# The last layer of a four-layer graph network: neighbours summed first, the first group's four parts in turn, output by node residue

## Chip, cores, metric

One core of a Trainium2 chip. In the views PE is TensorE's matmuls, PEld its weight loads, DVE VectorE, ACT ScalarE and POOL GpSimd.

## The reference

Four graph layers run over x of 128 graphs x 64 nodes x 256 features, each as layernorm(x + layer(x)). The change touches only the fourth:

```python
h = relu(einsum('ts,bsh->bth', adj, x @ Wg0 + bg0))
h = relu(einsum('ts,bsh->bth', adj, h @ Wg1 + bg1))
for p in range(1, 5):               # an LSTM over windows of p nodes
    nw   = 64 // p
    last = lstm_last(Wih[p-1], Whh[p-1], ..., h[:, :nw*p].reshape(-1, p, 256))
    h    = h.at[:, arange(nw)*p + p-1].set(last)
x = layernorm(x + h)
```

The sum over neighbours (`adj`) and the product with `Wg0` are linear, so adj (x Wg0 + bg0) = (adj x) Wg0 + rowsum(adj) bg0. The neighbours may be summed first.

After p = 3, nodes 0, 1 and 2 of every four are final. Only node 3 of every four is still written, by p = 4.

## The kernel before

Layer 3 (the fourth) runs in eight groups of 16 graphs. A group's graph convolution is a generator `gcn(g, a)` with four parts, a = 0 to 3, of 256 rows (4 graphs) each. Its steps are handed out one by one beside the LSTM of the group before. `bdT` is the adjacency, transposed, twice on a diagonal. x3, the layernorm's result, lies in a buffer that the views call A. Cuts are marked `# ...`.

```python
def gcn(g, a):
    # ... load x2r; z = A * sc2 + sh2 (ScalarE)
    # transpose z (L753), x2r += z (L754), layernorm on GpSimd -> x3 (L96), x3 to DRAM
    yield
    p_ = gbank([KD, 2, P])
    for k in range(KD):
        for c in range(2):
            nc.tensor.transpose(p_[:, k, c, :], x3[:, c, k*P:(k+1)*P], ident)      # L764
    hT = work.tile([P, KD, HT], F32, name="hT")
    nc.vector.tensor_copy(hT, p_.rearrange("p k c t -> p k (c t)"))
    yield
    for n in range(2):
        # hT x wg[n], 128x256 (L772); + bg[n] -> y (VectorE)
        yield
        # y x bdT, 128x128 (L780); relu -> hT (n = 0) or H (n = 1, L789)
        yield
GCN_STEPS = 6

def final(g):                                # four output tiles, by time
    # ... for a in range(4): load x3r, transpose H (L859), add, layernorm, store
    yield

for _ in steps_of(0):                        # first group: parts (0,1), then (2,3)
    pass
for g in range(NG):
    ending = final(g - 1) if g else iter(())
    side = steps_of(g + 1) if g + 1 < NG else iter(())
    n_side, done = halves * GCN_STEPS, 0     # 24
    for u, _ in enumerate(lstm(g)):          # 22 units: p = 1: 4, p = 2: 4, p = 3: 6, p = 4: 8
        next(ending, None)
        while done < min(n_side, (u + 1) * n_side / (n_units - 2)):
            next(side, None); done += 1
for _ in final(NG - 1):
    pass
```

## Time and profile before

| | before |
|---|---|
| time, median of 3 runs | 2362.1 us (2361.1 to 2364.0) |
| span of the profiled run | 2361.3 us |
| TensorE busy | 95% |
| end of layer 2 | 896.3 us |
| start: from there to the first LSTM matmul | 51.8 us |
| groups 0 to 6, start to start | 171.6, 178.1, 176.4, 178.1, 176.4, 178.1, 178.1 us |
| last group, to its last hidden state | 152.1 us |
| tail: from there to the end | 24.1 us |

The group starts are where the first 512-column LSTM matmul begins in the trace of TensorE.

### The profile page before, as it was taken

How to read it: one execution, taken by the hardware profiler on the slowest of the kernel's cores; microseconds unless marked ns; L12 is line 12 of the kernel's file. 1: busy time of each engine (PE TensorE's matmuls, PEld its weight loads, DVE VectorE, ACT ScalarE, POOL GpSimd, SP SyncE). 2: the span in 40 equal slices, each digit the busy share in tenths (PEclk: the TensorE clock that was granted, in tenths of full speed). 3: DMA queues.
4: the chain of work that ended last, by engine and by line, in shares of the span. 5: the costliest groups of instructions: out<-in, count | busy, mean ns of one | idle time of the engine just before them, and what ended most of it. 6: DMA issues, size and time to landing. Idle time of an engine off the chain costs nothing.

```text
span 2361.3 us, 25955 instructions
## 1 busy us (share of the span) xinstructions
PE 2239.4 (95%) x9673; PEld 1541.9 (65%) x9673; DVE 1019.8 (43%) x2320; ACT 910.8 (39%) x1885; POOL 408.1 (17%) x531
## 2 busy tenths in 40 slices
PE   5999999999899996999999999999999999999996
PEld 3767787778654444568568568568568568568475
DVE  5676766776744434322422422422422422422322
ACT  2565665566433801333333333333333333323331
POOL 1013333223320001010210210210210210210101
PEclk8899999999999997999999999999999999999998
DMA  3020222122223003000100100100100100100100
GB/s 119 10 38 29 46 57 39 38 46 39 30 47 90 0 0 116 18 18 1 54 18 1 54 18 1 54 19 1 54 18 1 54 18 1 45 10 1 36 1 27
DMA packets 126797, 74.75 MB, mean 32 GB/s; under 512 B 81872, under 2 KB 117328, under 8 KB 126416
## 3 DMA queue, kind: packets, MB, share of 16 engines
q1 hardware_dynamic: 124032, 70.22, 12.1%
q10 hardware_dynamic: 1616, 1.84, 0.2%
q8 instruction: 76, 1.25, 0.2%
q0 software_dynamic: 1024, 1.05, 0.2%
q14 instruction: 49, 0.40, 0.1%
HBM read 44.51 MB, written 28.57 MB: 31 GB/s over the span
## 4 chain that ended last, share of the span: by engine, by line
PE 87%; DVE 6%; ACT 3%; DMA 2%; POOL 2%; issue 1%; SPq 0%; POOLq 0%; ACTq 0%; DVEq 0%
PE l L818 32%; PE l L824 18%; PE g L772 5%; PE pz L680 5%; PE pz L616 5%; PE e L277 3%; PE g L780 2%; PE m L252 2%; PE m L365 2%; PE m L187 2%; PE z L286 2%; PE m L255 2%; PE m L377 1%; PE m L166 1%; DVE lo L290 1%
## 5 line engine op out<-in xcount | busy, mean ns | idle before, releaser
L818 PE MATMUL l<-H,wih 128*128 128x256 f32 (+2 forms) x2496 | 801.1, 472 | 0.3 <-DVE H L789 0.2
L818 PEld LDWEIGHTS l<-H,wih 128*128 128x128 f32 x2496 | 467.3, 191 | 246.2 <-issue 158.8
L824 PE MATMUL l<-hid,whh 128*128 128x256 f32 (+2 forms) x1536 | 435.9, 437 | 0.0
L824 PEld LDWEIGHTS l<-hid,whh 128*128 128x128 f32 x1536 | 291.8, 190 | 128.4 <-issue 61.2
L830 ACT ACTIVATE gate_i<-l,bias 128x256 f32<-128x256 f32 (+2 forms) x176 | 100.3, 570 | 646.2 <-PE l L824 514.9
L833 DVE TENSOR_TENSOR gate_i<-gate_i,gate_g 128x256 f32<-128x256 f32 (+2 forms) x96 | 47.8, 498 | 571.1 <-ACT gate_g L830 571.1
L834 POOL TENSOR_TENSOR cell<-gate_f,cell 128x256 f32<-128x256 f32 (+2 forms) x96 | 83.7, 872 | 1018.2 <-ACT gate_f L830 1018.2
L290 DVE SCALAR_TENSOR_TENSOR lo<-z,hi 128x512 fp32r<-128x512 f32 x256 | 167.4, 679 | 63.2 <-ACT hi L289 62.2
L289 ACT ACTIVATE hi<-z 128x512 fp32r<-128x512 f32 x256 | 143.7, 598 | 102.6 <-PE z L286 98.6
L82 POOL TENSOR_TENSOR ln_rs<-ln_rs,mhalf 128x2 f32<-128x2 f32 (+1 forms) x96 | 86.8, 904 | 520.3 <-DVE ln_ng L94 520.2
L830 ACT ACTIVATE gate_g<-l,bias 128x256 f32<-128x256 f32 (+2 forms) x176 | 100.2, 570 | 108.1 <-PE l L818 59.0
L830 ACT ACTIVATE gate_o<-l,bias 128x256 f32<-128x256 f32 (+2 forms) x176 | 99.5, 565 | 71.4 <-PE l L824 54.0
L277 PE MATMUL e<-lo,apad 128*128 128x512 f32 x256 | 110.7, 432 | 14.0 <-DVE lo L290 14.0
L772 PE MATMUL g<-wg,hT 128*128 128x256 f32 x512 | 122.6, 384 | 0.0
L286 PE MATMUL z<-gath_r,qs 128*128 128x512 f32 x256 | 109.9, 481 | 8.1 <-DVE lo L290 8.0
L837 DVE TENSOR_TENSOR cell<-gate_i,gate_g 128x512 f32<-128x512 f32 (+2 forms) x80 | 48.4, 604 | 154.6 <-ACT gate_g L830 154.5
L772 PEld LDWEIGHTS g<-wg,hT 128*128 128x128 f32 x512 | 98.3, 194 | 23.7 <-issue 10.5
L616 PE MATMUL pz<-A,w 128*128 128x512 f32 x256 | 112.7, 596 | 0.0
L277 PE MATMUL e<-hi,apad 128*128 128x512 f32 x256 | 108.3, 423 | 2.4 <-ACT hi L289 2.3
L838 ACT ACTIVATE gate_g<-cell 128x256 f32<-128x256 f32 (+2 forms) x176 | 89.9, 511 | 51.3 <-DVE cell L837 36.8
L843 DVE TENSOR_TENSOR H<-gate_o,gate_g 128x512 f32<-128x512 f32 (+2 forms) x80 | 47.6, 595 | 106.1 <-PE l L818 90.1
L616 PEld LDWEIGHTS pz<-A,w 128*128 128x128 f32 x256 | 48.2, 191 | 56.2 <-issue 55.0
(197 smaller groups left out, 2798.5 us busy)
## 6 DMA issues: line engine op xcount, KB each, us to landing
xin<-in_x SPq DMA_DIRECT2D x16, 512.0 KB
ld<-table SPq DMA_DIRECT2D x16, 512.0 KB
x_dram<-x SPq DMA_DIRECT2D x16, 512.0 KB
x2r<-x_dram SPq DMA_DIRECT2D x32, 256.0 KB
x_dram<-A SPq DMA_DIRECT2D x64, 128.0 KB
x3r<-x_dram SPq DMA_DIRECT2D x64, 128.0 KB
out<-st SPq DMA_DIRECT2D x64, 128.0 KB
wih<-in_WihT SPq DMA_DIRECT2D x3, 1024.0 KB
```

Source lines behind the costliest of these rows:

```text
L82: nc.gpsimd.tensor_tensor(dst, dst, mhalf[:, :n], OP.pow)
L277: nc.tensor.matmul(pes[S], apad[:, k, P - HEADS - r0:2 * P - HEADS - r0], t, start=first and n == 0, stop=False)
L286: nc.tensor.matmul(z, L1[q]["qs"][c][:, s, k * P:(k + 1) * P], gath_r, start=True, stop=True)
L289: nc.scalar.activation(hi, z, AF.Relu)
L290: nc.vector.scalar_tensor_tensor(lo, z, 0.0, hi.bitcast(F32), op0=OP.max, op1=OP.subtract)
L616: nc.tensor.matmul(p_, w1[:, k, m * P:(m + 1) * P], A[:, q, k * QT:(k + 1) * QT], start=k == 0, stop=k == KD - 1)
L680: nc.tensor.matmul(p_, w2[:, k, m * P:(m + 1) * P], hidden(q, k), start=k == 0, stop=k == M1 - 1)
L772: nc.tensor.matmul(p_[:, c, :], hT[:, k, c * P:(c + 1) * P], wg[n][:, k, :], start=k == 0, stop=k == KD - 1)
L818: nc.tensor.matmul(gates[n], wih[p][:, k, mw * P:(mw + 1) * P], Hw[:, k, :, s, :], start=k == 0, stop=not s and k == KD - 1)
L824: nc.tensor.matmul(gates[n], whh[p][:, k, m * P:(m + 1) * P], hid[:, k], start=False, stop=k == KD - 1)
L830: nc.scalar.activation(act[n], gates[n], AF.Tanh if n == "g" else AF.Sigmoid, bias=bias[:, p - 1, m:m + 1])
L838: nc.scalar.activation(act["g"], cell[:, j], AF.Tanh)
```

## The change

The intent has three parts. Drop the four transposes of x3 by multiplying with `bdT` first: a matmul with x3 as the stationary operand both sums neighbours and transposes (a part's eight records take 0.89 us within the groups). Run the first group's four parts in turn, where TensorE would otherwise wait for each pair. Put out three quarters of each group during its own p = 4 stage, so that one tile is left at the end. Cut to its core:

```diff
+    rb = we.tile([P, KD, 2, P], F32, name="rb")          # rowsum(adj) * bg0
+    ones = we.tile([P, P], F32, name="ones")
+    nc.vector.memset(ones, 1.0)
+    pr = gbank([P])
+    nc.tensor.matmul(pr, ones, bdT, start=True, stop=True)
...
-                nc.tensor.transpose(p_[:, k, c, :], x3[:, c, k * P:(k + 1) * P], ident)
+                nc.tensor.matmul(p_[:, k, c, :], x3[:, c, k * P:(k + 1) * P], bdT, start=True, stop=True)
+        hT = work.tile([P, KD, HT], F32, name="hT", bufs=3)
...
+                nc.tensor.matmul(p_[:, m, :], wg[0][:, k, m * P:(m + 1) * P], hT[:, k, :], ...)
+        nc.vector.tensor_add(hT, p_, rb.rearrange("p k c t -> p k (c t)"))
+        nc.scalar.activation(hT, hT, AF.Relu)
...                                     # then wg[1] and bdT as before
-    GCN_STEPS = 6
+    GCN_STEPS = 5
...
-    def final(g):
+    def final(g, s, pieces=1):          # the nodes s of every four
+        # s = 3: h is the last LSTM's own output; else GpSimd copies it out of H
...
-            parts = [gcn(g, a), gcn(g, a + 1)]
+        n = 2 if g else halves
+            parts = [gcn(g, a + m, gbank if g or m % 2 else lbank) for m in range(n)]
...
+            if u == 0 and g:
+                final(g - 1, SKIP - 1)
+            s, odd = divmod(u - first4, 2)          # u = 14, 16, 18
+            if not odd and 0 <= s < SKIP - 1:
+                final(g, s)
...
-    for _ in final(NG - 1):
-        pass
+    final(NG - 1, SKIP - 1, pieces=2)
```

`gbank` hands out the PSUM banks of the convolution, `lbank` those of the LSTM, which are free before the first group.

More of the change, by code (lines that the diff above doesn't have):

```diff
@@ L84, in layernorm @@
     def layernorm(dst, src, n, engine):
-        st = small.tile([P, n, 6], F32, name=f"ln_st{n}")
-        mv = small.tile([P, n, 2], F32, name=f"ln_mv{n}")
-        ng = small.tile([P, n], F32, name=f"ln_ng{n}")
-        rs = small.tile([P, n], F32, name=f"ln_rs{n}")
+        st = small.tile([P, n, 6], F32, name="ln_st", bufs=6)
+        mv = small.tile([P, n, 2], F32, name="ln_mv", bufs=6)
+        ng = small.tile([P, n], F32, name="ln_ng", bufs=6)
+        rs = small.tile([P, n], F32, name="ln_rs", bufs=6)
         for r in range(n):
@@ L644 @@
         wg = [weights(wd, f"wg{n}", i[f"L3_gnn_Wg{n}"]) for n in range(2)]
-        bg = [bcast(wd, f"bg{n}", i[f"L3_gnn_bg{n}"]) for n in range(2)]
+        bg0 = vec("bg0", i["L3_gnn_bg0"], KD)
+        bg1 = bcast(wd, "bg1", i["L3_gnn_bg1"])
         wih, whh = {}, {}
@@ L736, in gbank, with lbank, gcn @@
         return ps.tile([P] + shape, F32, name="g", bufs=3)
-    Hs = {}
-    def gcn(g, a):
+    def lbank(shape):
+        return ps.tile([P] + shape, F32, name="l", bufs=5)
+    rb = we.tile([P, KD, 2, P], F32, name="rb")
[3 more added lines that the diff above has]
+    nc.tensor.matmul(pr, ones, bdT, start=True, stop=True)
+    for k in range(KD):
+        for c in range(2):
+            nc.vector.tensor_scalar_mul(rb[:, k, c, :], pr, bg0[:, k:k + 1])
+    Hs, lasts = {}, {}
+    def gcn(g, a, bank):
         q, hf = divmod(g * halves + a, 2)
@@ L749, in gcn @@
                                  bias=sh2[:, m:m + 1], scale=sc2[:, m:m + 1])
-        p_ = gbank([2, D])
-        for c in range(2):
-            for m in range(KD):
+        p_ = bank([2, D])
+        for m in range(KD):
+            for c in range(2):
                 nc.tensor.transpose(p_[:, c, m * P:(m + 1) * P], z[:, m, c * P:(c + 1) * P], ident)
@@ L760, in gcn @@
         yield
-        p_ = gbank([KD, 2, P])
+        p_ = bank([KD, 2, P])
+        for c in range(2):
+            for k in range(KD):
+                nc.tensor.matmul(p_[:, k, c, :], x3[:, c, k * P:(k + 1) * P], bdT, start=True, stop=True)
+        hT = work.tile([P, KD, HT], F32, name="hT", bufs=3)
+        nc.vector.tensor_copy(hT, p_.rearrange("p k c t -> p k (c t)"))
+        yield
+        p_ = bank([KD, HT])
+        for m in range(KD):
+            for k in range(KD):
+                nc.tensor.matmul(p_[:, m, :], wg[0][:, k, m * P:(m + 1) * P], hT[:, k, :],
+                                 start=k == 0, stop=k == KD - 1)
@@ new lines, in gcn @@
+        hT = work.tile([P, KD, HT], F32, name="hT", bufs=3)
+        nc.vector.tensor_add(hT, p_, rb.rearrange("p k c t -> p k (c t)"))
+        nc.scalar.activation(hT, hT, AF.Relu)
+        yield
+        p_ = bank([2, D])
+        for c in range(2):
+            for k in range(KD):
+                nc.tensor.matmul(p_[:, c, :], hT[:, k, c * P:(c + 1) * P], wg[1][:, k, :],
+                                 start=k == 0, stop=k == KD - 1)
+        y = work.tile([P, 2, D], F32, name="st", bufs=5)
@@ L762, in gcn @@
+        nc.vector.tensor_add(y, p_, bg1[:, None, :].to_broadcast([P, 2, D]))
+        yield
+        p_ = bank([KD, 2, P])
         for k in range(KD):
             for c in range(2):
-                nc.tensor.transpose(p_[:, k, c, :], x3[:, c, k * P:(k + 1) * P], ident)
-        hT = work.tile([P, KD, HT], F32, name="hT")
-        nc.vector.tensor_copy(hT, p_.rearrange("p k c t -> p k (c t)"))
-        yield
-        for n in range(2):
-            p_ = gbank([2, D])
-            for c in range(2):
-                for k in range(KD):
-                    nc.tensor.matmul(p_[:, c, :], hT[:, k, c * P:(c + 1) * P], wg[n][:, k, :],
-                                     start=k == 0, stop=k == KD - 1)
-            y = work.tile([P, 2, D], F32, name="st", bufs=5)
-            nc.vector.tensor_add(y, p_, bg[n][:, None, :].to_broadcast([P, 2, D]))
-            yield
-            p_ = gbank([KD, 2, P])
-            for k in range(KD):
-                for c in range(2):
-                    nc.tensor.matmul(p_[:, k, c, :], y[:, c, k * P:(k + 1) * P], bdT, start=True, stop=True)
-            if n == 0:
-                hT = work.tile([P, KD, HT], F32, name="hT")
-                nc.vector.tensor_scalar_max(hT, p_.rearrange("p k c t -> p k (c t)"), 0.0)
-            else:
-                if g not in Hs:
-                    Hs[g] = work.tile([P, KD, N, GB], F32, name="H")
-                dst = Hs[g].rearrange("p k t b -> p k b t")[:, :, a * 4:(a + 1) * 4, :]
-                nc.vector.tensor_scalar_max(dst, p_.rearrange("p k c (s t) -> p k (c s) t", s=2), 0.0)
-            yield
@@ L792 @@
-    GCN_STEPS = 6
+                nc.tensor.matmul(p_[:, k, c, :], y[:, c, k * P:(k + 1) * P], bdT, start=True, stop=True)
+        if g not in Hs:
+            Hs[g] = work.tile([P, KD, N, GB], F32, name="H")
+        dst = Hs[g].rearrange("p k t b -> p k b t")[:, :, a * 4:(a + 1) * 4, :]
+        nc.vector.tensor_scalar_max(dst, p_.rearrange("p k c (s t) -> p k (c s) t", s=2), 0.0)
+        yield
+    GCN_STEPS = 5
     def lstm(g):
@@ L806, in lstm @@
                     last = s == p - 1
-                    new = None if last else work.tile([P, KD, nww, GB], F32, name="hid")
+                    over = last and p < SKIP
+                    if over:
+                        new = None
+                    elif last:
+                        new = work.tile([P, KD, nww, GB], F32, name="hd", bufs=3)
+                    else:
+                        new = work.tile([P, KD, nww, GB], F32, name="hid")
                     ends = []
@@ L842, in lstm @@
                             for jj, o, t in ends:
-                                nc.vector.tensor_mul(Hw[:, jj, :, s, :] if last else new[:, jj], o, t)
+                                nc.vector.tensor_mul(Hw[:, jj, :, s, :] if over else new[:, jj], o, t)
                         yield
                     hid = new
-    def final(g):
-        H = Hs.pop(g).rearrange("p k t b -> p k (t b)")
-        rows = [v[g * GB:(g + 1) * GB].rearrange("b (c t) d -> c t b d", t=TC) for v in (x3_dram, out_view)]
-        for a in range(halves):
-            xr = work.tile([P, 2, D], F32, name="x3r")
-            for c in range(2):
-                nc.sync.dma_start(xr[:, c, :], rows[0][2 * a + c])
+        lasts[g] = hid
@@ new lines, in final @@
+    def final(g, s, pieces=1):
+        if s == SKIP - 1:
+            h = lasts.pop(g)
+        else:
+            h = work.tile([P, KD, N // SKIP, GB], F32, name="hd", bufs=3)
+            nc.gpsimd.tensor_copy(h, Hs[g].rearrange("p k (w s) b -> p k w s b", s=SKIP)[:, :, :, s, :])
+        h = h.rearrange("p k w b -> p k (w b)")
+        rows = [v[g * GB:(g + 1) * GB].rearrange("b (c w s) d -> s c w b d", c=2, s=SKIP)[s]
+                for v in (x3_dram, out_view)]
+        xr = work.tile([P, 2, D], F32, name="x3r")
+        for c in range(2):
+            nc.sync.dma_start(xr[:, c, :], rows[0][c])
+        o = work.tile([P, 2, D], F32, name="st", bufs=5)
+        for cs in ([(0, 1)] if pieces == 1 else [(0,), (1,)]):
@@ L855, in final @@
             p_ = gbank([2, D])
-            for c in range(2):
-                t0 = (2 * a + c) * P
+            for c in cs:
                 for k in range(KD):
-                    nc.tensor.transpose(p_[:, c, k * P:(k + 1) * P], H[:, k, t0:t0 + P], ident)
-            nc.vector.tensor_add(xr, p_, xr)
-            o = work.tile([P, 2, D], F32, name="st", bufs=5)
-            layernorm(o, xr, 2, nc.gpsimd)
-            for c in range(2):
-                nc.sync.dma_start(rows[1][2 * a + c], o[:, c, :])
@@ L865, in final @@
-            yield
+                    nc.tensor.transpose(p_[:, c, k * P:(k + 1) * P], h[:, k, c * P:(c + 1) * P], ident)
+            r = slice(cs[0], cs[-1] + 1)
+            nc.vector.tensor_add(xr[:, r], p_[:, r], xr[:, r])
+            layernorm(o[:, r], xr[:, r], len(cs), nc.gpsimd)
+            for c in cs:
+                nc.sync.dma_start(rows[1][c], o[:, c, :])
     def steps_of(g):
-        for a in range(0, halves, 2):
-            parts = [gcn(g, a), gcn(g, a + 1)]
+        n = 2 if g else halves
@@ L871, in steps_of @@
+        for a in range(0, halves, n):
+            parts = [gcn(g, a + m, gbank if g or m % 2 else lbank) for m in range(n)]
             for _ in range(GCN_STEPS):
@@ L878 @@
     n_units = sum(-(-(N // p) // (QT // GB)) * p * KD for p in range(1, SKIP + 1))
+    first4 = n_units - SKIP * KD
     for g in range(NG):
-        ending = final(g - 1) if g else iter(())
         side = steps_of(g + 1) if g + 1 < NG else iter(())
@@ L884 @@
         for u, _ in enumerate(lstm(g)):
-            next(ending, None)
+            if u == 0 and g:
[3 more added lines that the diff above has]
+                final(g, s)
             while done < min(n_side, (u + 1) * n_side / (n_units - 2)):
```

## The prediction

> **What bounds the kernel now.** I read the page first, then the chain of work that ended last in order of time, then TensorE's waits, then the table by stretch. Shares say TensorE:
>
> ```profile
> PE 2239.4 (95%) x9673; PEld 1541.9 (65%) x9673; DVE 1019.8 (43%) x2320; ACT 910.8 (39%) x1885; POOL 408.1 (17%) x531
> PE 87%; DVE 6%; ACT 3%; DMA 2%; POOL 2%; issue 1%; SPq 0%; POOLq 0%; ACTq 0%; DVEq 0%
> ```
>
> An average does not say what the change is worth, since it touches only layer 3, which starts where layer 2's last matmul (L680) ends, at 896.3 us. In order of time, layer 3 has three parts. A *start* from 896.3 to 948.1, with no LSTM yet: four parts of the first group go through the graph convolution in two pairs. Then eight *groups* of LSTM, whose first matmuls begin at 948.1, 1119.9, 1298.0, 1474.5, 1652.6, 1829.0, 2007.2 and 2185.3. Last a *tail*, from the last hidden state at 2337.2 to 2361.3. The start, from the chain:
>
> ```profile
> 897.91 9.11 DMA x2r<-x_dram
> ...
> 914.59 4.52 PE g L772 x16
> 919.11 1.94 PE g L780 x16
> 921.05 3.46 PE g L772 x16
> 924.51 2.01 PE g L780 x16
> ...
> 932.96 1.11 POOL A L96 x2
> ...
> 947.01 1.04 DVE H L789
> ```
>
> The reader is to see that the second pair (from about 926) runs the whole chain again, with its own wait for GpSimd's normalisation, and that the same 16 records cost 4.52 us after a pause and 3.46 later. Within a group TensorE is nearly full, so what matters there is matmul time and holes. The chain gives the unit costs (two records per f32 matmul, one per transpose), and the waits give the one hole:
>
> ```profile
> 1202.11 0.89 PE g L780 x8
> ...
> 1221.96 0.44 PE g L764 x4
> ...
> 1240.92 1.73 PE g L772 x8
> ```
>
> ```profile
> PE g L764 <- POOL A L96: 9.6, 5, 1.9
> ```
>
> That is the wait table from 1145 on; a sixth such wait of 1.9 us falls at 1133. Each sits near a group's start, where the scheduler put the transposes of x3 (L764) only about 2.5 us behind those of z (L753), while the residual add, the statistics and GpSimd's normalisation take 5.5 us. The hole costs more than itself. In the table by stretch around four of the six holes:
>
> ```profile
> 1134.00:1145.00 11.00, 10.14 (x29) 5.30 (x30) 6.39 (x20) 3.27 (x5) 5.84 (x9) 0.84 0.44 131
> 1311.00:1322.00 11.00, 9.09 (x31) 4.70 (x31) 7.45 (x24) 3.40 (x6) 7.23 (x11) 1.00 0.49 142
> 1489.00:1500.00 11.00, 10.57 (x30) 5.51 (x31) 6.09 (x20) 3.27 (x5) 5.30 (x10) 0.84 0.46 143
> 1665.00:1676.00 11.00, 9.09 (x31) 4.51 (x30) 8.01 (x28) 3.96 (x7) 7.14 (x10) 1.00 0.47 141
> ```
>
> After the window come its length, then PE busy; the clock is the third number from the end. Where it is 0.84, the same work takes more PE time. The groups agree: from start to start they last 178.1, 176.4, 178.1, 176.4, 178.1 and 178.1 us, the long ones being those with a lowered clock (0.84 twice above; the other two show 0.84 and 0.86). So the drop costs 1.7 us, in four of six.
>
> [...]
>
> **The change, part by part.** The order of instructions up to layer 2's end is the same in both kernels but for one tiny load, so 896.3 stays.
>
> *Neighbours first.* Per part (256 rows) the old path has 4 transposes of z, 4 of x3, 8 wide matmuls and 8 matmuls with bdT. The new one multiplies x3 by bdT directly, which sums and transposes at once: 4 transposes, 8 wide, 8 with bdT. Exactly the 4 transposes of L764 go: 0.44 us. VectorE loses one 128x512 pass (0.69 us) and ScalarE gains a Relu, both beside TensorE. Seven groups of parts (those for groups 1 to 7) lie on TensorE's path: 7 x 4 x 0.44 = 12.4 us.
>
> *The holes.* In the new order the z transposes of a first part are followed by 2 LSTM matmuls, the second part's transposes and 6 more (1.72 + 0.44 + 5.15 = 7.3 us) before x3 is used, against the 5.5 us needed; only one output tile is at work then, not four. I expect the holes and drops to go: 6 x 1.9 + 4 x 1.7 = 18.2 us.
>
> *Four parts in turn.* TensorE reaches x3 of the first part at 911.3 as now. GpSimd's normalisations come every 1.86 us (0.70 + 1.10 and gaps), so the fourth is done near 917.4, its bdT matmuls at 918.0. Then 4 x 1.73 (wg0) + 4 x 1.73 (wg1) + 4 x 0.89 (bdT) = 17.4, plus some 1.2 for the cold clock (4.52 against 3.46), ends at 936.6; VectorE's four writes of H at 1.04 to 1.07 us, begun at 934.2, end at 938.4. The LSTM starts there, not at 948.1: 9.7 us. Buffers: three hT make a copy wait for the first wg0 product, which TensorE's 1.73 us per part covers.
>
> *Output by residue.* Three of a group's four output tiles move into its own p = 4 stage. The count is the same, but three of group 0 now lie within the counted groups: 3 x 0.44 = 1.3 us lost. The larger effect is the tail. Before:
>
> ```profile
> 2337.26 0.56 PE g L859 x3
> ...
> 2346.04 4.03 DMA x3r<-x_dram
> ...
> 2356.16 0.54 POOL st L96
> ```
>
> Four tiles, the later two waiting for x3r, because two buffers are reloaded only after the first outputs: 24.0 us from the hidden state to the end. After: one tile in two halves, its x3r loaded long before. Transposes and add 0.9, statistics and the two small operations 0.85, power and normalisation 1.25 give 3.0 for the first half, 4.3 for the second (one more GpSimd power and normalisation), then 4.6 from the last normalisation to the end as now (2356.7 to 2361.3): 8.9 us. Gain 15.1.
>
> *Sum:* 12.4 + 18.2 + 9.7 - 1.3 + 15.1 = 54.1; 2362.1 - 54.1 = 2308.0 us.
>
> **Rivals.** *Holes move.* In the new order the filler between the last p = 3 product and the first p = 4 product is 0.89 us of bdT work instead of 1.73, and a residue copy on GpSimd must end before the transposes behind the first p = 4 unit. For it: a hole of 1 us in seven groups with a clock drop in four costs about 14 us, giving 2322. Against: in the last group, which has no filler at all there, 2288.5 to 2297.45 holds 8.64 us of matmuls, a stall of 0.3 us; and the permuting copy of 128x1024 took 2.03 us, so 128x512 is estimated at 1.0 us, with 3.5 us from the p = 3 end to its use. ScalarE's Relu could also wait for VectorE and hold back gates, but ScalarE is 33% busy in these groups.
>
> *Only matmul time goes.* If the holes persist in another place and the start is bound by the GpSimd chain with a cold clock throughout (gain 6), it is 12.4 - 1.3 + 6 + 15 = 32, or 2330: within 2%. For it: holes depend on a scheduler's order, which I judge by arithmetic. Against: the 2 us of margin.
>
> *The start is limited by the loads.* x2r lands at 907 because weights go ahead of it on the same queue; it still does, and parts 3 and 4 might come later than I think. The DMA rate falls off after 908, so all four loads should be there by 910, and this is hidden behind GpSimd's rate.
>
> **Range and chances.** 2% faster is 2314.9, so I have 7 us in hand. The tail (15) and the transposes (12) are almost certain, the start sure to 3 us; the 18 us of holes carry the doubt. Half of them surviving gives 2317. Better than 2300 needs slack that I do not see: the records of a full group alone (LSTM 147.9: 136 records of 512 columns at 0.429, 152 of 336 at 0.283, 216 of 256 at 0.216; convolution 4 x 5.68; output 1.7) come to 172.3 us, against 176.4 - 1.9 - 1.8 = 172.7 in my sum. Range 2300 to 2320; faster 0.8, same 0.19, slower 0.01.
>
> **What would show it.** Group length 172 to 173 us, all alike, with no TensorE wait on A at group starts and the clock at 1.00 there; first LSTM matmul near 938; no L764-like transposes; tail near 9 us with no DMA wait in it. Groups of 174 or more, or waits on hd or H at the p = 4 start, would show the first rival. A start above 942 would break the part-in-turn step.

## More of the kernel before

The metric is device microseconds of one execution.

The prediction shows the lines for the start, the waits and the tail, so here is only one hole in detail. The view is TensorE's timeline in the kernel before; columns are start, length, engine, line and operation. The profile models where a matmul ends, and lengths run into the next start (1308.32 plus 0.60 is past 1308.76), so differences of starts say more.

```profile
1306.88 0.75 PE L753 MATMUL g<-ident,st 128*128 128x128 f32 x4
1307.46 1.02 PE L818 MATMUL l<-H,wih 128*128 128x512 f32 x2
1308.32 0.60 PE L753 MATMUL g<-ident,st 128*128 128x128 f32 x4
1308.76 1.02 PE L818 MATMUL l<-H,wih 128*128 128x512 f32 x2
1309.62 0.60 PE L859 MATMUL g<-ident,H 128*128 128x128 f32 x4
1310.06 1.02 PE L818 MATMUL l<-H,wih 128*128 128x512 f32 x2
1312.99 0.33 PE L764 MATMUL g<-ident,A 128*128 128x128 f32 x1 [1.91 <-POOL A L96]
```

The z transposes of the first part are issued by 1307.46. The x3 transposes, which need VectorE's add and statistics and GpSimd's normalisation first, start at 1312.99, 5.53 us later. Only 3.62 us of TensorE work stand between, so TensorE idles 1.91.

## The result

2309.8 us median (2308.6 to 2310.3, 4 runs) against 2362.0 on the same chip. The ratio is 0.9777, 95% interval 0.976 to 0.9794: faster, by 2.2%. Ratios are the mean of one kernel's runs over the mean of the other's in the same rounds, so not quite the ratio of the medians. The predicted time was 2308.0.

From the page of the changed kernel, busy times and the chain's shares:

```profile
PE 2217.8 (96%) x9547; PEld 1526.4 (66%) x9547; DVE 1000.6 (43%) x2296; ACT 928.2 (40%) x1917; POOL 417.9 (18%) x556
PE 89%; DVE 5%; ACT 3%; DMA 1%; POOL 1%; issue 1%; SPq 0%; POOLq 0%; ACTq 0%; DVEq 0%
```

TensorE still sets the time, with 21.6 us less of busy time. The start, from the chain of work:

```profile
911.29 0.57 POOL A L96
...
911.90 2.08 PE l L779 x8
913.98 1.86 PE g L779 x8
915.84 1.77 PE l L779 x8
917.61 1.13 PE g L779 x8
918.74 1.73 PE l L786 x8
...
933.49 3.72 DVE H L808 x4
...
937.25 7.99 PE l L844 x18
```

There is one run through the convolution where the kernel before had two. The four bdT products start 1.86 us apart, as GpSimd's normalisations do, and from 918.74 TensorE runs without a gap. TensorE's waits from 940 to the end (waited for, total, times, longest):

```profile
PE g L893 <- DVE hd L869: 1.4, 1, 1.4
PE l L844 <- ACT gate_g L864: 0.5, 1, 0.5
```

The six waits for A are gone. The first of these two lies in the tail and the second at 2168.7, in the last group. One of the stretches where z and x3 stand now, in the table by stretch (PE busy comes after the length, the clock is the third number from the end):

```profile
1118.00:1129.00 11.00, 11.00 (x39) 5.86 (x38) 6.74 (x19) 5.90 (x11) 4.80 (x8) 1.00 0.44 131
```

TensorE is busy for all 11 us, at full clock. The tail, from the chain:

```profile
2299.10 0.44 DVE hd L869
...
2302.37 0.56 POOL st L96
2302.92 0.52 POOL ln_rs L82
```

No read of x3r is left in it. By part, from the two profiled runs:

| part | predicted gain | before | after | measured gain |
|---|---|---|---|---|
| end of layer 2 | 0 | 896.3 | 896.7 | -0.4 |
| start | 9.7 | 51.8 | 40.6 | 11.2 |
| group 0 (4 x 0.44, less 1.3) | 0.5 | 171.6 | 171.7 | -0.1 |
| groups 1 to 6 (transposes 10.6, holes and clock 18.2) | 28.8 | 1065.4 | 1038.0 | 27.4 |
| last group | 0 | 152.1 | 152.5 | -0.4 |
| tail | 15.1 | 24.1 | 8.3 | 15.8 |
| sum | 54.1 | 2361.3 | 2307.9 | 53.4 |

The parts are rounded one by one.

### The profile page after: what moved, and what is told of

The parts are those of the page before. It is cut to its first block, busy times and chain, and to the rows that moved or that the text cites.

```text
span 2307.9 us, 25661 instructions
## 1 busy us (share of the span) xinstructions
PE 2217.8 (96%) x9547; PEld 1526.4 (66%) x9547; DVE 1000.6 (43%) x2296; ACT 928.2 (40%) x1917; POOL 417.9 (18%) x556
## 4 chain that ended last, share of the span: by engine, by line
PE 89%; DVE 5%; ACT 3%; DMA 1%; POOL 1%; issue 1%; SPq 0%; POOLq 0%; ACTq 0%; DVEq 0%
PE l L844 33%; PE l L850 18%; PE pz L681 5%; PE pz L616 5%; PE e L277 3%; PE m L252 2%; PE m L187 2%; PE m L365 2%; PE g L786 2%; PE g L795 2%; PE z L286 2%; PE m L255 2%; PE m L377 1%; PE g L779 1%; PE m L166 1%; PE g L803 1%
## 5 line engine op out<-in xcount | busy, mean ns | idle before, releaser
L82 POOL TENSOR_TENSOR ln_rs<-ln_rs,mhalf 128x2 f32<-128x2 f32 (+2 forms) x97 | 84.5, 871 | 544.1 <-DVE ln_ng L94 543.4
L869 DVE TENSOR_TENSOR H<-gate_o,gate_g 128x512 f32<-128x512 f32 (+1 forms) x64 | 40.9, 639 | 87.7 <-PE l L844 70.1
L856 ACT ACTIVATE gate_f<-l,bias 128x256 f32<-128x256 f32 (+2 forms) x96 | 51.1, 532 | 60.2 <-PE l L850 60.2
L263 DVE TENSOR_TENSOR qs<-m,qs 64x256 fp32r<-64x256 f32 x128 | 53.9, 422 | 48.2 <-ACT qs L262 46.2
```

What stands on the lines that cost most here:

```text
L82: nc.gpsimd.tensor_tensor(dst, dst, mhalf[:, :n], OP.pow)
L856: nc.scalar.activation(act[n], gates[n], AF.Tanh if n == "g" else AF.Sigmoid, bias=bias[:, p - 1, m:m + 1])
```

## The experiments

Theory: the gain is a sum of four causes that can be undone one by one. These are the x3 transposes, the start in one run, the tail with one tile, and holes closed by wider spacing of the side steps. The main rival concerns the holes: they went because the output tiles went away, or because of the convolution's new form. The runs were made on several chips: beside them the kernel before took 2360.9 us (first four runs below), 2361.7 (next four) and 2358.3 (last two), so differences of a few us between chips are read from the parts of the profiles and not from the times.

### The old kernel with another spacing

```diff
-            while done < min(n_side, (u + 1) * n_side / (n_units - 2)):
+            while done + 1 <= min(n_side, (u + 1) * n_side / (n_units - 2)):
```

> The kernel before with one thing changed: the side steps of the next group's convolution are handed out with the count rounded down (one step beside the first LSTM unit, not two), so x3 of the first part is used some 8 us of TensorE work after its z transposes, not 2.5. Theory (the holes at group starts are a matter of spacing, and each drop of the clock follows from a hole): the six holes of 1.9 us and the four clock drops of 1.7 us go, groups last 174.5 us all alike, time 2362 - 18 = 2344 us. Rival (the holes come from four output tiles crowding VectorE and GpSimd there): holes of at least 1 us remain, time 2352 or more.

Measured: 2346.0 us, ratio 0.9931 (0.9914 to 0.9947). Groups 1 to 6 last 174.6 or 174.7 us each, 17.5 us less in sum than before, and between the groups' first and last starts TensorE waits for nothing but 0.2 us at the first LSTM matmul. The steps keep their rate, and each comes later by up to one unit. TensorE's timeline:

```profile
1131.35 1.88 PE L818 MATMUL l<-H,wih 128*128 128x512 f32 x4
...
1139.53 0.60 PE L764 MATMUL g<-ident,A 128*128 128x128 f32 x4
```

x3 is used 8.2 us after the z transposes, and nothing waits, with all four output tiles in place. One line of the old kernel thus gives what I had booked under the change. The profiled run is 15.8 us shorter than that of the kernel before, not 17.5, because it left layer 2 at 897.4, took 52.2 us for its start and 0.6 more for group 0, and 0.4 less for its tail; the medians differ by 14.9.

### Neighbours first alone, at two spacings

Both are the kernel before with the new convolution in it, the first group in pairs and the old output. The second also keeps the old rate:

```diff
-            while done < min(n_side, (u + 1) * n_side / (n_units - 2)):
+            while done < min(n_side, (u + 1) * 24 / (n_units - 2)):
```

> The kernel before with only the neighbours-first convolution (five steps per part, so also one side step per LSTM unit), first group in pairs and output as before. Theory: 28 parts x 0.44 = 12.4 us of transposes go from the groups, some 2 us from the start's two pairs, and the holes and clock drops (18 us) go because five steps are spaced wider: 2362 - 32 = 2330 us, groups 172.7 us. Rival (the holes need the output moved away): holes stay, 2348 us.

> As e2, but the side steps at the old rate of 1.2 per LSTM unit. Theory (spacing): x3 of the first part is used some 3.5 us after its z transposes again, the holes of about 2 us come back with some clock drops, only the transposes' 14 us are gained: 2348 us, groups 174.5 to 176.5. Rival (the convolution's new form itself removes the holes): 2330 us as e2.

Measured: 2327.7 us, ratio 0.9854 (0.9837 to 0.987), with no waits for A in the groups, and 2344.4 us, ratio 0.993 (0.9913 to 0.9946), with six waits of 1.9 to 2.0. The holes came back with the old rate, so the rival that the new form removes them fell. The first kernel's groups last 172.7 to 172.9, 1.9 us under those of the spacing experiment; predicted were 4 x 0.44 = 1.8. Its start takes 48.4 us instead of 51.8: the new convolution alone shortens the chain of two pairs by 3.4. In two of the second kernel's six groups the clock fell as well, to 0.84 in the stretch around the hole (176.6 us; the others 174.9 to 175.0). Around two of the holes:

```profile
1302.00:1313.00 11.00, 9.06 (x37) 5.32 (x37) 7.52 (x24) 3.06 (x6) 6.83 (x10) 1.00 0.49 151
1477.00:1488.00 11.00, 9.09 (x33) 5.29 (x33) 6.26 (x19) 2.68 (x5) 5.87 (x9) 0.84 0.49 152
```

### The changed kernel with the old output, and with the old spacing

The first puts `final` back as in the kernel before. The second changes only the rate, with the same edit as above.

> The changed kernel with the output as before (four tiles by time at the next group's start, four at the end). Theory: the tail is 24 us again, not 8.4, and group 0 loses three tiles' 1.3 us; holes stay away since the spacing is the new one: 2310 + 14 = 2324 us. Rival (the holes went because the output moved): 2342 us with waits for A at group starts.

> The changed kernel with side steps at the old rate of 1.2 per LSTM unit: x3 of the first part is used 3.9 us after its z transposes, with only one output tile near. Theory (spacing): TensorE waits for A some 1.6 us at each of six group starts, with clock drops in some: 2320 to 2327 us. Rival (crowding by output tiles, which are away here): no holes, 2310 us.

Measured: 2320.4 us, ratio 0.9823 (0.9807 to 0.984), and 2317.0 us, ratio 0.9811 (0.9796 to 0.9826). With four output tiles at each group's start and the new spacing TensorE waits for nothing there, and the groups last 172.7 to 172.8 us. With the tiles away and the old spacing six holes are back:

```profile
1116.58 1.02 PE L844 MATMUL l<-H,wih 128*128 128x512 f32 x2
1117.44 0.60 PE L767 MATMUL g<-ident,st 128*128 128x128 f32 x4
1117.87 2.74 PE L844 MATMUL l<-H,wih 128*128 128x512 f32 x6
1122.10 1.25 PE L779 MATMUL g<-bdT,A 128*128 128x128 f32 x8 [1.49 <-POOL A L96]
```

Both rivals fell: output tiles neither make the holes nor close them. The time from the z transposes to x3's use says why:

| kernel | output tiles near | TensorE work between | hole | sum |
|---|---|---|---|---|
| before | 4 | 3.62 | 1.91 | 5.53 us |
| neighbours first, old rate | 4 | 3.61 | 1.91 | 5.52 us |
| changed, old rate | 1 | 4.03 | 1.49 | 5.52 us |
| changed | 1 | 7.3 | none | |
| before, new spacing | 4 | 8.2 | none | |

Add, statistics and normalisation take 5.5 us in all three kernels with holes, with four output tiles near or one, and a hole is what TensorE's own work leaves of it. The 1.49 us holes cost only themselves: all six groups last 174.5 us, with the clock at 1.00 in the six stretches around them. One of the stretches:

```profile
1120.00:1131.00 11.00, 9.51 (x35) 5.06 (x34) 4.14 (x11) 3.51 (x6) 4.24 (x6) 1.00 0.35 114
```

In the kernel before, half clock followed four of the six holes of 1.91 us: from 1135.08 to 1138.49, 1490.07 to 1493.48, 1845.05 to 1848.47 and 2022.55 to 2025.96, 3.41 us each. Half of that is the 1.7 us by which the groups differ. The first of these stretches and the 3.41 us before it, in its table by stretch:

```profile
1131.67:1135.08 3.41, 1.50 (x8) 0.67 (x7) 3.41 (x14) 1.30 (x2) 2.48 (x3) 1.00 0.32 105
1135.08:1138.49 3.41, 3.41 (x8) 1.76 (x8) 1.25 (x3) 0.69 (x1) 2.03 (x4) 0.50 0.58 165
```

The 3.41 us before each of the four hold a whole hole: TensorE is busy for 1.50 us in all four. Every change of the granted clock in this trace lies a whole number of 3.41 us from 1135.08. Counted in such steps, one hole without a drop lies across an edge (1311.08 to 1312.99, edge at 1311.80), and the other ends on one (1667.56). Drops came with four of six holes in the kernel before, with two of six in neighbours first at the old rate, and with none of the six of 1.49 us. Whether their length or their place spared these is not shown.

The old output's tail is 23.7 us, 15.4 more than 8.3. The time came out 3.6 us under the expectation, which already held the 1.3 us of group 0 (170.4 against 171.7). In the profiled runs the six full groups are 0.25 us shorter each than the changed kernel's 173.0 (1.5 in sum), the last group is 0.4 shorter, layer 2 ended 0.7 earlier, and the tail came out 0.3 under the 24 expected. The 0.25 us are a small hole that the change did move. Where p = 2 begins in the changed kernel, a weight load waits 0.83 us for VectorE's last write of H from p = 1 (it ends at 1306.72 in one group), and two matmul records take 0.60 and 0.53 us instead of 0.43, in groups 0 to 6 alike. With the old output the four transposes of an output tile (0.43 us) come just before, and the two records are short; in its group 0, which has no such tile, they are long again. TensorE's list of waits shows none of this, since the records count as busy; its weight loads do, in the timeline of the changed kernel:

```profile
1306.77 0.30 PEld L844 LDWEIGHTS l<-H,wih 128*128 128x128 f32 x2 [0.83 <-DVE H L869]
```

So groups 1 to 6 gain 17.5 us by spacing and 11.2 by the convolution (1047.9 less 1036.7 us, in the two old-output kernels without holes). Less some 1.3 for this they give the 27.4.

### The first group in pairs

```diff
-        n = 2 if g else halves
+        n = 2
```

> The changed kernel with the first group's parts in two pairs. Theory: the start (layer 2's end to the first LSTM matmul) takes 49 to 50 us, not 40.5, everything after is as in the changed kernel: 2310 + 9 = 2319 us. Rival (the start is bound by the load of x2r and the cold clock, so pairs cost little): 2312 us.

Measured: 2315.2 us, ratio 0.9804 (0.9789 to 0.9819). The start takes 47.4 us, the groups 173.0 as in the changed kernel, and TensorE waits twice for A (8.3 and 4.3 us) instead of once. So the four parts in turn are worth 6.8 us, not the 9.7 I gave them. Of the other 4.4 of the start's 11.2 us the new convolution alone brought 3.4; what brings the last 1.0 no run separates.

### The last tile in one piece

```diff
-    final(NG - 1, SKIP - 1, pieces=2)
+    final(NG - 1, SKIP - 1)
```

> The changed kernel with the last output tile in one piece. Theory (halves overlap VectorE's and GpSimd's work): tail 9 to 9.5 us, not 8.4; 2310.5 us. Rival (the power on GpSimd costs nearly the same for one column as for two, so halves gain nothing): same time or up to 0.5 us less.

Measured: 2308.5 us, ratio 0.9777 (0.9764 to 0.9791), not to be told from the changed kernel's 0.9777. The tail is 8.7 us against 8.3. In two halves the last normalisation ends 4.57 us after the hidden state, in one piece 4.5. GpSimd's power takes 0.55 us for one column and 0.70 for two (1.22 for four), so a second power eats what the halves gain. What is left, 0.4 us of a shorter last store in the profile, is not seen in the times. The theory of overlap fell; the gain of the tail is that of fewer tiles.

### Two cuts more in the start

In the changed kernel the first x2r lands at 907.4, 9.07 us after its issue, behind weights that are needed only at p = 3 and 4. The first kernel issues those weights after the first group's reads:

```diff
-    for p in (3, 4):
-        wih[p] = weights(we, f"wih{p}", i["WihT"][p - 1])
-        whh[p] = weights(we, f"whh{p}", i["WhhT"][p - 1])
...
+    for n, _ in enumerate(steps_of(0)):
+        if n == halves - 1:
+            # the same four loads here
```

> The changed kernel with the weights of p = 3 and 4 issued behind the first four reads of x2r, not ahead. Theory: the first x2r lands near 900 and not at 907.4; then the last normalisation constant (900.3) and the z transposes (to about 902.9) bound the start, so the LSTM starts 4 to 5 us earlier: 2305 us. Rival: GpSimd's normalisations or the weights (now landing beside x3's writes) take the place: 2309 us or more.

Measured: 2302.9 us, ratio 0.9756 (0.9742 to 0.9769), with a start of 34.8 us instead of 40.6: 5.8 us less where 4 to 5 were expected. Its chain has no DMA wait any more:

```profile
898.38 0.16 DVE sh L601
898.54 0.15 DVE ones L742
...
900.70 0.61 DVE x2r L765
```

The last normalisation constant now releases the start, and behind it come `ones` and the bias products. The second kernel has GpSimd set `ones` and lets VectorE normalise every other part of the first group; the first one was run again beside it on the same chip:

```diff
-    nc.vector.memset(ones, 1.0)
+    nc.gpsimd.memset(ones, 1.0)
-        layernorm(x3, x, 2, nc.gpsimd)
+        layernorm(x3, x, 2, nc.gpsimd if g or a % 2 == 0 else nc.vector)
```

> The same kernel as e7_x2r_first, for a comparison on the chip of e9: 2303 us, start 34.8 us.

> e7 with two more cuts in the start: VectorE normalises x3 of the first group's second and fourth part, so GpSimd's row of 1.86 us per part is halved, and the ones for the bias matmul are set by GpSimd early, so TensorE doesn't wait 4.2 us for VectorE. Theory: the fourth part's x3 is ready 2 us earlier, start 32.5 to 33 us, time 2301 us. Rival (VectorE, which also has the adds, statistics and copies there, becomes the bound): start 34.5 to 36 us, 2303 us or more.

Measured: 2299.4 us (2298.9 to 2302.2), ratio 0.9751, and 2297.0 us (2296.4 to 2297.8), ratio 0.974 (0.9724 to 0.9757). The four runs of each do not overlap, but the intervals of their ratios do, so the step is small. The starts of the two profiled runs were 36.5 and 33.9 us, but the first is the slowest of its four runs, and the half clock ended 18.2 us after layer 2 in it (from 909.02 six records with wg0 still took 2.55 us) and 13.2 in the other (from 905.82 ten took 2.16). Beside the 34.8 us of the same kernel's earlier run, where it ended after 13.4, the gain is 0.9: less than the 2 us of the theory, more than its rival's none. GpSimd's memset ran right behind its power for the normalisation constants, so the wait for `ones` only fell from 4.2 to 3.6 us. How much each half of the edit brought, no run separates. With 2297.0 this version beats both kernels.

## Why the prediction was right

*What bounds the kernel.* TensorE, read in order of time rather than by share. It stayed the bound (89% of the chain), and the sum of parts came out at 53.4 us against 54.1. That it came so close is in part luck: the start gave 1.5 us more and the tail 0.7 more than predicted, groups 1 to 6 gave 1.4 less, group 0 0.6 less, and layer 2's end and the last group 0.4 less each.

*Neighbours first.* 0.44 us per part: the two convolutions at equal spacing differ by 1.9 us a group against 1.8. In the profile four transposes of 128x128 take 0.44 us, four matmuls of that size (eight records with bdT) 0.89. The part that I missed is the start, which it shortens by 3.4 us. I had booked the whole start under "four parts in turn".

*The holes.* 18.2 predicted, 17.5 measured in the spacing experiment. The arithmetic, 7.3 us of work against 5.5 us needed, was the cause. The half sentence that only one output tile is at work then was not: with four it needs the same 5.5. One reading was wrong: behind the z transposes of the old kernel I counted about 2.5 us of work, and it is 3.62, which with the hole of 1.91 makes the 5.5.

*Clock drops.* 1.7 us each, gone with the 1.9 us holes. That the six holes of 1.49 us brought none I had not foreseen. It is one reason why the changed kernel with the old spacing ended at 2317 and not above 2320; its layer 2 also ended 1.5 us earlier.

*Four parts in turn.* The start ended 1.5 us shorter than I said, and partly by luck: the step named here is worth 6.8 us, and the convolution's 3.4, not counted here, made up for it. In the sum for the new start two terms were too long: the four writes of H (3.72 us against 4.2) and the 1.2 us for a cold clock in the first wide products (before, 4.52 us at a granted clock of 0.77 against 3.46 at 1.00). The table by stretch of the changed kernel shows where the low clock fell, 0.60 in the first stretch and 1.00 in the second:

```profile
911.90:918.70 6.80, 6.80 (x33) 6.54 (x34) 4.21 (x17) 0.00 (x0) 5.76 (x10) 0.60 0.59 185
918.70:925.60 6.90, 6.90 (x34) 6.07 (x33) 2.08 (x3) 1.26 (x2) 0.00 (x0) 1.00 0.49 143
```

It lay on the bdT products, which GpSimd paces anyway (the last one starts at 917.49, just behind its first normalisation at 917.45); the wide products ran at full clock, 1.73 us each from the first.

*Tail.* 8.9 predicted, 8.3 measured. The last normalisation ends 4.6 us after the hidden state, where 4.3 was predicted, and the rest to the end takes 3.8 and not 4.6. The halves, which this counted on, gain nothing that the times show.

*The rivals.* No hole moved to where I feared it: the first p = 4 unit shows no wait, and GpSimd's copies took 0.62 us each (estimated 1.0) and TensorE never waited for them. The 0.25 us per group at the start of p = 2 were overlooked; as a place for a moved hole I had named only p = 4. ScalarE's Relus (32 of 0.63 us) held back nothing that TensorE waited for, and took no table load of their own: both kernels have four, of 1.28 us each. The loads of x2r were hidden from the second part on: VectorE waited for one only, 4.7 us. That first one, 9.07 us from issue to landing, did set the start of the chain, which the load order then improved.

## What to carry to other kernels

A producer that returns to TensorE through other engines needs enough TensorE work behind it, here 5.5 us. Count that work in the instruction order and set the spacing on purpose, since here a change in the number of steps moved it by accident and paid a third of the gain. When several edits come together, undo them one at a time: the largest term needed one line of the old kernel. At a stage's start, look at which transfers stand ahead of the first needed one in the same queue: here their order was worth 5.8 us.
